# Layer 1 of a four-layer graph network: fill in chunk order, own rows fetched later, score rows spread inside the loop, last block in halves

## The chip, the cores and the metric

The kernel runs on one core of a Trainium2 chip. The core has a matrix engine (TensorE, PE in the profile; its weight loads are shown as PEld), three engines for elementwise work (VectorE = DVE, ScalarE = ACT, GpSimd = POOL), a sync engine (SP) that issues transfers, and 16 DMA engines that move the data. Each engine works through its own queue of instructions in order and waits on semaphores for the others. POOL also issues the indirect transfers, which gather rows by a list of indices.

The metric is the device time of one execution in microseconds (us), as the median of several runs. Lower is better.

## The reference

A matrix `x` of 2708 nodes by 512 features goes through four layers over the same sparse adjacency matrix `adj` (2708 x 2708, about four neighbours per node besides the diagonal). Each layer is followed by `x = layernorm(x + layer(x))`. The change concerns layer 1:

```python
def _L1_gnn_ref(x, adj_a, adj_b, W_sa, a_sa, W_gcnb, b_gcnb, Wa, ba, Wb, bb):
    type_sum_a = adj_a @ x
    type_sum_b = adj_b @ x
    attn_a = sigmoid(concat([type_sum_a, x], 1) @ Wa.T + ba)
    attn_b = sigmoid(concat([type_sum_b, x], 1) @ Wb.T + bb)
    h = x @ W_sa
    s_left, s_right = h @ a_sa[0, :Hd], h @ a_sa[0, Hd:]
    scores = s_left[:, None] + s_right[None, :]
    e = where(adj_a != 0, exp(-leaky_relu(scores, 0.01)), 0.0)
    x_a = (e / (e.sum(1, keepdims=True) + 1e-05)) @ h
    x_b = adj_b @ (x @ W_gcnb) + b_gcnb
    return sigmoid(attn_a * x_a + attn_b * x_b)
```

Layers 0, 2 and 3 are a graph convolution, a hypergraph mean and a symmetrically normalized convolution with a tanh.

## The kernel before, in words

**Tiling.** The nodes are cut into NB = 24 blocks of R = 113 rows. For each block the kernel holds a list of at most 512 edges, in EC = 4 chunks of 128. One chunk is one indirect transfer (`gather`, L604): 128 partitions each receive the table row of one edge's source node. The sum over neighbours is then four matmuls per output half, one per chunk, with a 128 x 113 matrix that has each edge's value (or score) at the column of its target row.

**Layer 1's table.** Layer 0 ends by writing `table[0]` to DRAM: for each node 1029 numbers (4116 bytes), that is `h`, `x @ W_gcnb`, and a few columns for the scores and gates. `store0` writes its windows; the last one, of 20 rows, is the last thing that layer 0 puts there. Layer 1 then needs, for every block, four gathered chunks (into one of NGB = 3 buffers `gath`) and the block's own rows of the table (diagonal terms), which lie in one of NO = 9 places (`own_place`). `load_own1` fetches own rows with plain transfers from SP's queue; `gather_own1` (L1396) does so with one indirect transfer from POOL's queue.

**The fill.** In layer 0's last steps the own rows of blocks 0 to 3, then 4 to 6 are fetched by `load_own1`, and after the last `store0` those of blocks 7 and 8. Then come set-up operations on VectorE (`ediag`, `gates`, `inverse`, `in_block`, `block_of`), `gather1(0)` and `gather1(1)` on POOL, the edge matrices of both blocks on ScalarE (`values1`), and six `spread_left` (L1376 on): each takes the column `s_left` of four blocks and spreads it by four PE transposes (L1380) into a PSUM tile `sl`, from which VectorE copies it (L1383) as a row over all partitions. There are two such PSUM buffers. `spread_bias` (L1559, L1560) does the same for the bias. Then `scores1(0)` (L1424 to L1429) and `mask1(0)` (L1434) make the scores of block 0.

**The loop.** The schedule is written by hand (`manual_schedule`): each engine runs its instructions in program order. Step i does, in this order:

- `gather1(i + 2)` on POOL;
- `sums1(i)` on PE (L1441, tile `l1s`): the plain sums, first all four chunks of the first output half, then of the second;
- `both1(i - 1)` on VectorE (L1486 to L1497, tiles `rec`, `l1a`, `l1v`) and a tanh on ScalarE (L1501): it joins the two branches of the block before;
- `scored_sums1(i)` on PE (L1451, tile `l1e`). There is one PSUM buffer for it, so it waits for `l1a` of block i - 1;
- `scores1(i + 1)`, which needs all four chunks of block i + 1;
- `gather_own1(i + 8)` on POOL for steps 1 to 15;
- `stats1(i - 1)` (L1506 to L1522; in every second step POOL raises the variances of two blocks to the power -0.5, L1523);
- `gates1(i)` and `gated1(i)` (L1461 to L1480, tile `l1b`): ScalarE copies two columns to `row_cnt` (L1465) ahead of the long VectorE operation L1471;
- `mask1(i + 1)`, `scale1`, `norm1(i - 2)`, whose rows SP stores to `table[1]`, and `source_sum(i)` (L1352), a small VectorE operation.

**The end.** After step 23 `both1(23)`, `stats1(23)`, `norm1(23)` finish the last block: VectorE and ScalarE take turns on tiles 512 wide. Layer 2 gathers from `table[1]`, so its first gather waits for the last store.

Of the kernel before, what the change touches and what calls it, by code (L numbers as in the profile page):

```python
# [447 lines left out]
def sparse_stack(  # L448
# [199 lines left out]
    def load_own1(i):  # L648
        r = rows(i)
        own1[i] = own_place(i)  # L650
        move_rows(
            r, lambda a, b: own1[i][a:b, 1 : 2 * D + 1],
            lambda a, b: table[0][i * R + a : i * R + b, 1 : 2 * D + 1],
        )
# [7 lines left out]
    with ExitStack() as phase:  # L662
# [632 lines left out]
                    load_own1(i)  # L1295
        keep_busy(4)
        store0(KB - 1)
        for i in range(7, NO):
            load_own1(i)


    gpool = ctx.enter_context(tc.tile_pool(name="gpool", bufs=1))
# [26 lines left out]
    for k, t in enumerate((ba_bc, bb_bc)):  # L1329
# [4 lines left out]
    nc.vector.reciprocal(inverse, inverse)  # L1334


    in_block = gpool.tile([P, NB, NS], I32, name="in_block")
    nc.vector.tensor_scalar(
        in_block, where_all, 1.0 / R, 0.5 / R - 0.5, op0=ALU.mult, op1=ALU.add
    )  # L1340
    block_of = gpool.tile([P, NB, NS], FP, name="block_of")
    for g, (c0, _) in enumerate(SEGS):
        at = slice(8 * g, 8 * g + 8)
        nc.vector.tensor_scalar(
            block_of[:, :, at], in_block[:, :, at], float(c0), None, op0=ALU.add
        )
    deg_k = gpool.tile([P, KB], FP, name="deg_k")

    def source_sum(b):
# [68 lines left out]
                bias=edges[:, i, c, 1:2], scale=nvalue[:, i, c : c + 1],  # L1418
            )

    def scores1(i):

        e = spool.tile([P, EC, R], FP, tag="e", name=f"e{i}")
        nc.vector.tensor_tensor(  # L1424
            e, gath[i % NGB][:, :, SR : SR + 1].to_broadcast([P, EC, R]),
            over_chunks(s_left[:, i, :]), ALU.add,
        )
        nc.vector.scalar_tensor_tensor(e, e, 0.01, e, op0=ALU.mult, op1=ALU.max)
        nc.scalar.activation(e, e, AF.Exp, scale=-1.0)  # L1429
        edge_e[i] = e  # L1430

    def mask1(i):
        e = edge_e[i]
        nc.vector.scalar_tensor_tensor(e, edge_s[i], 0.0, e, op0=ALU.is_gt, op1=ALU.mult)  # L1434

    def sums1(i):
        g, s, r = gath[i % NGB], edge_s.pop(i), rows(i)
        sum_s[i] = ps_1s.tile([P, 2, D], FP, tag="s1", name=f"l1s{i}")
        for k, at in enumerate(s_at):
            for c in range(EC):  # L1440
                nc.tensor.matmul(  # L1441
                    sum_s[i][:r, k, : at.stop - at.start], lhsT=s[:, c, :r], rhs=g[:, c, at],
                    start=(c == 0), stop=(c == EC - 1),
                )

    def scored_sums1(i):
        g, e, r = gath[i % NGB], edge_e.pop(i), rows(i)
        sum_e[i] = ps_1e.tile([P, 2, D], FP, tag="e1", name=f"l1e{i}")
        for k, at in enumerate(e_at):
            for c in range(EC):  # L1450
                nc.tensor.matmul(  # L1451
                    sum_e[i][:r, k, k : k + at.stop - at.start], lhsT=e[:, c, :r],
                    rhs=g[:, c, at], start=(c == 0), stop=(c == EC - 1),
                )

    def gates1(i):

# [21 lines left out]
        )  # L1479
        nc.scalar.activation(vb[:r, :], vb[:r, :], AF.Copy, scale=gate[:r, 1:2])  # L1480

    def both1(i):

        r, agg = rows(i), sum_e.pop(i)
        rec = small.tile([P, 1], FP, tag="rec", name=f"rec{i}")
        nc.vector.scalar_tensor_tensor(  # L1486
            rec[:r, :], agg[:r, 0, 0:1], 1e-5, ediag[:r, i : i + 1], op0=ALU.add, op1=ALU.add
        )
        nc.vector.reciprocal(rec[:r, :], rec[:r, :])
        nc.vector.tensor_mul(rec[:r, :], rec[:r, :], gate1.pop(i)[:r, 0:1])  # L1490
        va = work.tile([P, D], FP, tag="u", name=f"l1a{i}")
        nc.vector.scalar_tensor_tensor(  # L1492
            halves(va, r), halves(own1.pop(i)[:, 1 : D + 1], r), ediag[:r, i : i + 1],
            agg[:r, :, 1 : H + 1], op0=ALU.mult, op1=ALU.add,
        )
        v = work.tile([P, D], FP, tag="v", name=f"l1v{i}")
        nc.vector.scalar_tensor_tensor(  # L1497
            v[:r, :], va[:r, :], rec[:r, :], vb1.pop(i)[:r, :], op0=ALU.mult, op1=ALU.add
        )

        nc.scalar.activation(v[:r, :], v[:r, :], AF.Tanh, scale=0.5)  # L1501
        v1[i] = v

    def stats1(i):
        r, v = rows(i), v1[i]
        nc.vector.scalar_tensor_tensor(  # L1506
            v[:r, :], v[:r, :], 0.5, xr[:r, i, :], op0=ALU.mult, op1=ALU.add
        )
        stats = small.tile([P, 6], FP, tag="stats", name=f"st_l1_{i}")
        nc.vector.bn_stats(stats[:r, :], v[:r, :])  # L1510
        k = i % 2
        if k == 0 or i >= NB - 2:
            mv2[0] = small.tile([P, 2, 4], FP, tag="mv4", name=f"mv_l1_{i}")
        mv = mv2[0]
        nc.vector.bn_aggr(mv[:r, k, 0:2], stats[:r, :])
        v1[i] = v, mv[:, k, :]
        if k == 0 and i < NB - 2:
            return

        at = slice(k, k + 1) if i >= NB - 2 else slice(0, 2)  # L1520
        n = at.stop - at.start
        nc.vector.tensor_scalar(mv[:r, at, 1], mv[:r, at, 1], 1e-5, None, op0=ALU.add)  # L1522
        nc.gpsimd.tensor_tensor(  # L1523
            mv[:r, at, 2], mv[:r, at, 1], root[:r, :].to_broadcast([r, n]), ALU.pow
        )
        unscaled[0] = r, mv, at
# [60 lines left out]

    plus = const.tile([P, NB], FP, name="plus")
    inv_norm = const.tile([P, NB], FP, name="inv_norm")
    nc.vector.tensor_scalar(plus, adiag, 0.0, None, op0=ALU.is_gt)  # L1590

    def row_norms(at, on_pool=True):
        n = at.stop - at.start
# [41 lines left out]
    values1(0, range(EC))  # L1635
    gather1(1)
    values1(1, range(EC))
    for i in range(0, NB, 4):
        spread_left(i)
    spread_bias(bg_bc)  # L1640
    scores1(0)
    mask1(0)
    for i in range(NB):
        if i + 2 < NB:
            gather1(i + 2)
        sums1(i)
        if i > 0:
            both1(i - 1)
        if i + 2 < NB:
            values1(i + 2, (0, 1))  # L1650
        scored_sums1(i)
        if i + 1 == NB:
            turn_norm(0)
            turn_norm(1)
        if i + 1 < NB:
            scores1(i + 1)
        if 0 < i and i - 1 + NO < NB:
            gather_own1(i - 1 + NO)
        if 0 < i < NB - 1:
            stats1(i - 1)  # L1660
        gates1(i)
        if i + 2 < NB:
            values1(i + 2, (2, 3))
        gated1(i)
        if i + 1 < NB:
            mask1(i + 1)
        else:
            stats1(i - 1)
        scale1()
        if i > 1:  # L1670
            norm1(i - 2)
        if i + 1 == NB:
            norm1(i - 1)
        if i + 1 == NB:
            nc.sync.dma_start(out=b3_bc[0:1, :], in_=b3[None, :])
            nc.sync.dma_start(out=w3_sb, in_=w3T.rearrange("(b p) o -> p b o", p=P))
        if i < KB:
            source_sum(i)
        if i == KB:
            source_sums_out()  # L1680
            row_norms(slice(0, KB))
    copy_norm(0)
    copy_norm(1)
    keep_warm(ps_sp, "sp", [P, 4, P], 8)
    both1(NB - 1)
    spread_row(b3_bc, "b3")
    stats1(NB - 1)
    scale1()
    norm1(NB - 1)
    deg_ps = source_sums_in()  # L1690
# [234 lines left out]
```

## Time and profile before

| | us |
|---|---|
| median of 3 runs | 958.26 (957.83 to 959.23) |
| the profiled execution | 958.69 |
| its span, first to last instruction | 956.9 |
| PE busy | 884.8 (92%) |
| VectorE busy | 685.3 (72%) |
| ScalarE busy | 526.3 (55%) |
| POOL busy | 465.5 (49%) |
| first gather of layer 1 issued | 414.26 |
| first scored sums of layer 1's last block | 603.17 |
| first gather of layer 2 issued | 618.51 |

The shares are means over stages with different limits: layer 0 fills the span to about 414 us, layer 1 goes to 618, layer 2 to about 760, layer 3 to the end. What the change is worth has to be read from the stage it touches. A line of the view in order of time has start, duration, engine, line of the kernel, operation, output<-input, shape, count, and in brackets the idle time of the engine ahead of it with what ended it. The list of waits has who waited for whom, microseconds in total, times, and the longest. `issue` means that the engine waited for nothing that the profile shows.

### The profile page before, as it was taken

The page shows a single profiled execution, that of the slowest core. Times are in us where ns is not written, and L with a number is a line of the kernel's source. Part 1 is how long each engine was busy: PE and PEld are TensorE (multiplying, and loading weights), DVE is VectorE, ACT ScalarE, POOL GpSimd, SP SyncE. Part 2 cuts the span into 40 slices and gives each one's busy share as a digit, 9 for nine tenths or more (in the row PEclk, how much of TensorE's full clock was granted, in tenths as well). Part 3 has the DMA queues.
Part 4 walks back from the last instruction along what each step waited for, and adds up shares of the span by engine and source line. Part 5 has one row for each costly group of instructions (what it writes and reads, how often), then busy time and mean ns, then how long its engine had stood idle before and what let it go on. Part 6 is the DMA issues. An engine that isn't in the chain of part 4 may idle for free.

```text
span 956.9 us, 11163 instructions
## 1 busy us (share of the span) xinstructions
PE 884.8 (92%) x2957; PEld 489.4 (51%) x2957; DVE 685.3 (72%) x1811; ACT 526.3 (55%) x1221; POOL 465.5 (49%) x518
## 2 busy tenths in 40 slices
PE   6889999999999999989999999798888899999993
PEld 2446565556565565557777777433233334444441
DVE  7788798888888853148999999777777436565553
ACT  5776676867677672347777777344544312222221
POOL 3323131432323230057777753377777477766630
PEclk7879999999999999989999999989999999999997
DMA  9986887988878454388999976367777466555531
GB/s 245 323 208 184 216 229 207 272 223 220 227 206 238 152 166 126 115 286 292 349 330 342 341 276 236 95 188 213 212 218 217 131 170 189 163 174 162 151 107 32
DMA packets 133717, 201.73 MB, mean 211 GB/s; under 512 B 82658, under 2 KB 82704, under 8 KB 133647
## 3 DMA queue, kind: packets, MB, share of 16 engines
q0 software_dynamic: 39024, 118.69, 40.2%
q1 hardware_dynamic: 94623, 82.25, 30.2%
q8 instruction: 26, 0.43, 0.2%
q14 instruction: 44, 0.36, 0.1%
HBM read 182.81 MB, written 27.80 MB: 220 GB/s over the span
## 4 chain that ended last, share of the span: by engine, by line
PE 58%; DMA 14%; DVE 14%; issue 5%; ACT 4%; SPq 3%; POOL 2%; POOLq 0%; DVEq 0%; ACTq 0%
PE o_l L588 15%; DMA gath<-table,source 11%; PE l3a L617 8%; PE hb L588 7%; PE h L588 7%; PE l0a L617 6%; PE l2a L617 2%; PE fetched L929 2%; POOL gath L604 2%; PE unread L1585 2%; DVE l1b L1471 1%; SPq L691 1%; DMA gath<-in_x_dram 1%; DVE l1b L1475 1%; DVE l1a L1492 1%
## 5 line engine op out<-in xcount | busy, mean ns | idle before, releaser
L604 POOL DMA_INDIRECT gath<-table,source x288 | 305.0, 1059 | 102.7 <-issue 49.0
L604 POOL DMA_INDIRECT gath<-in_x_dram,source x96 | 97.4, 1015 | 224.9 <-issue 190.7
L617 PE MATMUL l2a<-gath,s_left 128*113 128x512 f32 (+1 forms) x192 | 97.2, 624 | 17.6 <-DMA gath<-table,source 17.4
L1451 PE MATMUL l1e<-gath,e 128*113 128x257 f32 (+3 forms) x384 | 88.4, 383 | 10.4 <-DVE l1a L1492 10.4
L617 PE MATMUL l3a<-gath,s 128*113 128x512 f32 (+1 forms) x192 | 88.3, 603 | 2.7 <-DMA gath<-table,source 2.7
L1441 PE MATMUL l1s<-gath,s 128*113 128x256 f32 (+3 forms) x384 | 89.8, 387 | 0.0
L617 PE MATMUL l0a<-gath,s 128*113 128x512 f32 (+1 forms) x192 | 87.5, 596 | 0.1
L588 PE MATMUL o_l<-shared,xi_own 128*113 128x512 f32 (+1 forms) x192 | 86.5, 593 | 0.8 <-ACT xi_own L581 0.7
L588 PE MATMUL hb<-w_gc_sb,xi_own 128*128 128x512 f32 (+1 forms) x176 | 83.3, 601 | 0.0
L1451 PEld LDWEIGHTS l1e<-gath,e 128*113 128x113 f32 (+1 forms) x384 | 66.2, 177 | 32.7 <-PE l1s L1441 19.4
L588 PE MATMUL o_l<-w_sb,uw_own 128*128 128x512 f32 (+1 forms) x176 | 82.7, 614 | 0.2
L588 PE MATMUL h<-w_sa_sb,xi_own 128*128 128x259 f32 (+1 forms) x352 | 80.8, 382 | 0.0
L1441 PEld LDWEIGHTS l1s<-gath,s 128*113 128x113 f32 (+1 forms) x384 | 69.2, 181 | 17.8 <-ACT s L1416 1.5
L588 PEld LDWEIGHTS h<-w_sa_sb,xi_own 128*128 128x128 f32 (+1 forms) x352 | 64.8, 185 | 19.8 <-issue 6.1
L617 PEld LDWEIGHTS l2a<-gath,s_left 128*113 128x113 f32 (+1 forms) x192 | 30.4, 181 | 73.9 <-DMA gath<-table,source 53.9
L1844 ACT ACTIVATE y<-l3v,mv_l 113x512 f32<-113x512 f32 (+1 forms) x24 | 19.5, 813 | 86.2 <-DVE mv_l L1840 79.2
L588 PEld LDWEIGHTS o_l<-shared,xi_own 128*113 128x113 f32 (+1 forms) x192 | 33.9, 177 | 49.2 <-issue 47.1
L617 PEld LDWEIGHTS l0a<-gath,s 128*113 128x113 f32 (+1 forms) x192 | 33.5, 179 | 40.7 <-issue 35.5
L617 PEld LDWEIGHTS l3a<-gath,s 128*113 128x113 f32 (+1 forms) x192 | 32.5, 180 | 41.2 <-issue 37.9
L1818 DVE SCALAR_TENSOR_TENSOR l3v<-o_l,d_inv,b_bc 113x512 f32<-113x512 f32 (+1 forms) x25 | 18.1, 728 | 48.1 <-PE o_l L588 48.1
L1308 DVE TENSOR_SCALAR s<-niota_r,nrow,edges 128x113 f32<-128x113 f32 x192 | 51.5, 344 | 0.0
L876 DVE FIND_INDEX8 where_all<-rec_all,shared 128x8 uint32<-128x678 f32 (+1 forms) x64 | 51.2, 800 | 0.0
(256 smaller groups left out, 1580.6 us busy)
## 6 DMA issues: line engine op xcount, KB each, us to landing
shared<-in_adj_dram SPq DMA_DIRECT2D x14, 1186.5 KB
table<-st SPq DMA_DIRECT2D x21, 514.5 KB
gath<-in_adj_dram SPq DMA_DIRECT2D x7, 1186.5 KB
gath<-in_x_dram SPq DMA_DIRECT2D x21, 256.0 KB
xi_own<-in_x_dram SPq DMA_DIRECT2D x23, 224.0 KB
table<-xr SPq DMA_DIRECT2D x23, 224.0 KB
table<-y SPq DMA_DIRECT2D x23, 224.0 KB
out_dram<-y SPq DMA_DIRECT2D x23, 224.0 KB
```

The source lines that it names most:

```text
L588: nc.tensor.matmul(o, lhsT=uT[:, f, :r], rhs=w[:, f, :], start=(f == 0), stop=(f == DB - 1))
L604: nc.gpsimd.indirect_dma_start(out=g[:, c, :n], out_offset=None, in_=src[:, :], in_offset=bass.IndirectOffsetOnAxis(ap=source[:, i, c : c ...
L617: nc.tensor.matmul(agg[:r, :], lhsT=s[:, c, :r], rhs=g[:, c, off : off + D], start=(c == 0), stop=(c == EC - 1),)
L691: nc.sync.dma_start(out=a[:TAIL, NF, :r], in_=adjT[NF * P :, at])
L876: nc.vector.max_index(out=where_all[:, i, g * 8 : (g + 1) * 8], in_max=top, in_values=seg)
L929: nc.tensor.matmul(t["fetched"][:, c, : 3 * NS], lhsT=t["q"][:, c * P : (c + 1) * P], rhs=rec_all[:, i].rearrange("p k s -> p (k s)"), sta ...
L1308: nc.vector.tensor_scalar(s[:, c, :], niota_r, nrow[:, i, c : c + 1], edges[:, i, c, 1:2], op0=ALU.is_equal, op1=ALU.mult,)
L1441: nc.tensor.matmul(sum_s[i][:r, k, : at.stop - at.start], lhsT=s[:, c, :r], rhs=g[:, c, at], start=(c == 0), stop=(c == EC - 1),)
L1451: nc.tensor.matmul(sum_e[i][:r, k, k : k + at.stop - at.start], lhsT=e[:, c, :r], rhs=g[:, c, at], start=(c == 0), stop=(c == EC - 1),)
L1585: nc.tensor.matmul(o[:, :cols], lhsT=ident, rhs=bg_bc[:, :cols], start=True, stop=True)
L1818: nc.vector.scalar_tensor_tensor(v[:r, at], o[:r, at], d_inv[:r, i : i + 1], b3_bc[:r, at], op0=ALU.mult, op1=ALU.add,)
L1844: nc.scalar.activation(y[:r, :], v[:r, :], AF.Identity, bias=mv[:r, 3:4], scale=mv[:r, 2:3])
```

## The change

1. The plain transfers of the own rows of blocks 7 and 8 after the last `store0` go. `gather_own1` fetches six blocks ahead, so it starts with block 7 in step 1 and goes on to step 17.
2. `spread_left` runs for blocks 0 to 7 in the fill; the other four calls stand in steps 1 to 4 of the loop, ahead of `source_sum`.
3. Block 0's scores and masks are made in two halves (chunks 0 and 1, chunks 2 and 3), and its matmuls go chunk by chunk over both output halves. Other blocks keep their order.
4. `in_block`, `block_of` and `plus` are computed after `spread_bias`. Two matmuls whose result nobody reads stand ahead of `spread_bias`.
5. The last block's `both1` and `stats1` work on two halves of 256 columns.

Most of the diff's text only moves functions ahead of the fill. Its core:

```diff
         store0(KB - 1)
-        for i in range(7, NO):
-            load_own1(i)
...
-    def scores1(i):
+    def scores1(i, at=slice(0, EC)):
+        if i not in edge_e:
+            edge_e[i] = spool.tile([P, EC, R], FP, tag="e", name=f"e{i}")
+        e, n = edge_e[i][:, at, :], at.stop - at.start
...
-    def mask1(i):
+    def mask1(i, at=slice(0, EC)):
+        e = edge_e[i][:, at, :]
...
+    def in_turn(i, parts):
+        both = [(k, at, c) for k, at in enumerate(parts) for c in range(EC)]
+        return sorted(both, key=lambda t: t[2]) if i == 0 else both
...
-        for k, at in enumerate(s_at):
-            for c in range(EC):
+        for k, at, c in in_turn(i, s_at):
...
-    def both1(i):
+    def both1(i, parts=2):
+        for k in range(0, 2, parts):
+            kk, at = slice(k, k + parts), slice(k * H, (k + parts) * H)
+            nc.vector.scalar_tensor_tensor(
+                halves(va, r)[:, kk, :], halves(own, r)[:, kk, :], ediag[:r, i : i + 1],
+                agg[:r, kk, 1 : H + 1], op0=ALU.mult, op1=ALU.add,
+            )
+            nc.vector.scalar_tensor_tensor(
+                v[:r, at], va[:r, at], rec[:r, :], vb[:r, at], op0=ALU.mult, op1=ALU.add
+            )
+            nc.scalar.activation(v[:r, at], v[:r, at], AF.Tanh, scale=0.5)
...
-    def stats1(i):
+    def stats1(i, parts=1):
+        for k in range(parts):
+            at = slice(k * D // parts, (k + 1) * D // parts)
+            nc.vector.scalar_tensor_tensor(
+                v[:r, at], v[:r, at], 0.5, xr[:r, i, at], op0=ALU.mult, op1=ALU.add
+            )
+            nc.vector.bn_stats(stats[:r, k, :], v[:r, at])
...
-    for i in range(0, NB, 4):
+    for i in (0, 4):
         spread_left(i)
+    unread = ps_1s.tile([P, 2, D], FP, tag="s1", name="unread")
+    for _ in range(2):
+        nc.tensor.matmul(
+            unread[:, 0, :], lhsT=ident[:R, :], rhs=xr[:R, 0, :], start=True, stop=True
+        )
     spread_bias(bg_bc)
...
-    scores1(0)
-    mask1(0)
+    for at in (slice(0, 2), slice(2, EC)):
+        scores1(0, at)
+        mask1(0, at)
     for i in range(NB):
...
-        if 0 < i and i - 1 + NO < NB:
-            gather_own1(i - 1 + NO)
+        if 0 < i and i + 6 < NB:
+            gather_own1(i + 6)
...
+        if 0 < i and 4 * i + 4 < NB:
+            spread_left(4 * i + 4)
         if i < KB:
             source_sum(i)
...
-    both1(NB - 1)
+    both1(NB - 1, 1)
     spread_row(b3_bc, "b3")
-    stats1(NB - 1)
+    stats1(NB - 1, 2)
```

## The prediction

> **What bounds the kernel now.** The profiled execution took 958.69 us, of which 956.9 are span and 1.8 lie around it; the median of the runs shown is 958.26 (957.83 to 959.23). I add my terms to 958.69 and move the result down by 0.43 to stand beside the median. One execution differs from the next by about 0.2%, so below 0.2% (1.9 us) I call a difference "within".
>
> The change touches layer 1 alone: its fill (from about 414 to 434 us), its loop of 24 blocks (to about 604) and its last block (to 617). I read the loop first, in the view of stages (us, then busy us of PE, PE's weight loads, VectorE, ScalarE, POOL, PE clock, DMA share, GB/s), and in the list of waits between 430 and 600 us (who waited for whom, us in total, times, longest).
>
> ```profile
> 430.00:550.00 120.00, 113.17 (x507) 88.11 (x506) 109.21 (x283) 91.24 (x232) 92.16 (x86) 1.00 0.94 331
> 550.00:596.00 46.00, 43.13 (x194) 33.63 (x193) 42.05 (x110) 35.66 (x91) 23.66 (x24) 1.00 0.77 266
> ```
> ```profile
> PE l1e L1451 <- DVE l1a L1492: 9.7, 22, 0.6
> DVE l1b L1471 <- ACT row_cnt L1465: 7.7, 23, 0.7
> ```
>
> VectorE is busy 91% in both stretches, and the only idle time that the list gives it is the 0.3 us a step in which ScalarE reads `row_cnt`. It never waits for a transfer or for PE; PE waits for VectorE, 22 times. In the instructions in order of time, `l1a` (L1492) starts at 449.41 and 456.89: the step is 7.5 us, 7.8 in the next, 15.3 for two. Own-row fetches stop at 545 us, POOL's work and the DMA share fall, and the pace stays: POOL's pair-wise power op starts at 537.87, 553.14 and 568.46. So **VectorE sets the loop**, and whatever is added to its queue there is paid.
>
> The fill is the opposite. In order of time (start, duration, engine, line, in brackets the idle time before it):
>
> ```profile
> 414.26 1.01 POOL L604 DMA_INDIRECT gath<-table,source  x1 [0.43 <-issue]
> ...
> 416.20 1.16 DVE L1383 COPY s_left<-sl 128x452 f32<-128x452 f32 x2
> ...
> 419.06 0.63 DVE L1383 COPY s_left<-sl 128x452 f32<-128x452 f32 x1 [0.33 <-PE sl L1380]
> ...
> 423.34 0.99 POOL L604 DMA_INDIRECT gath<-table,source  x1 [0.30 <-issue]
> 424.33 0.63 DVE L1424 TENSOR_TENSOR e<-gath,s_left 128x452 f32<-128x452 f32 x1 [1.52 <-DMA gath<-table,source]
> ...
> 429.35 0.63 DVE L1424 TENSOR_TENSOR e<-gath,s_left 128x452 f32<-128x452 f32 x1 [2.46 <-DMA gath<-table,source]
> ```
>
> VectorE waits here for transfers: 1.52 us for block 0's last chunk, 2.46 for block 1's. POOL issues a chunk every 1.3 us from 414.26 without a stop, the eighth at 423.34, and it lands 5.9 us later (median issue to landing of the eight: 5.9). From 429.35 VectorE runs through step 0 and reaches the first `l1a` at 434.17. **Only the landing of chunk 8 and VectorE's work behind it set the fill's end**; the sums of block 0 on PE are not on that path.
>
> **The change, part by part.**
>
> *Block 0 by chunks.* The sums of block 0 are put in chunk order, and its scores are made in two halves: three more VectorE operations, one more ScalarE. A half-length operation keeps a fixed part: in layer 3 the row of the 512-wide `l3v` has 0.751, of the 256-wide 0.477, so 2 x 0.477 - 0.751 = 0.2 fixed. Three of them are 0.6 us, in VectorE's 4.0 us of idle. On PE the first sums end earlier than 431.38 (where block 0's scored sums end now), but the next VectorE instruction that needs them comes after 429.35 anyway: the gate at 430.57 waits for nothing now, and the sums' first long user, at 431.43, waits for ScalarE. Gain 0; POOL's fetch of block 3, now held by 0.36 us at 430.36 for a buffer, starts at its usual 0.30, but no one waits for it. If the cover failed, 0.6 us.
>
> *Moved set-up.* `in_block` and `block_of` (0.50 and 0.83) go behind the bias copy, into the same idle time; four of the six spreads leave the fill, which makes room for them: 0. The two added unread matmuls stand on PE where it is idle for 2.45 us before 416.87: 0.
>
> *No own rows in the fill.* Four SP transfers go (two blocks, 0.93 MB, issued 411.44 to 412.79). They could hold up the chunks only by sharing the DMA engines. Bytes by queue between 415.3, when the first chunk's issue ends, and 417 us (q1 is SP's queue, q0 POOL's):
>
> ```profile
> q0 software_dynamic: 42, 0.17, 49.9%
> q1 hardware_dynamic: 58, 0.17, 36.9%
> ```
>
> After 416.5 q0 is alone. So 0.17 MB of own rows compete; at 0.33 MB/us (331 GB/s in the loop) that is 0.5 us. The bounds: 0, if the 5.9 us belong to the chunks themselves when they follow each other at 1.3 us (the fourth and the eighth both have it, though the own rows had long ended); 1.5, if all chunks came down to the 4.4 of the first chunk after a DMA pause, at 584.69. I take **-0.5**, since the bytes are what was seen. The tail of the table store, which releases POOL's queue at 413.56, was issued before those transfers and shares engines with them: 0 to -0.3, taken as 0.
>
> The Trainium skill, "DMA: Bandwidth & Descriptors", section "Anatomy of one DMA — SWDGE (gpsimd) path", gives about 2.0 us plus bytes over 436 GB/s for one such transfer. With 128 rows of 4116 bytes that is an estimate of 3.2 us, 4.2 with the 1.0 us of issue, where this trace has 5.9; by the rule the fill would gain 1.7 and not 0.5, and the whole sum would come out 1.2 lower.
>
> *Own rows six ahead.* Steps 1 to 15 issue one own fetch each, as before; steps 16 and 17 get one more each, 1.3 us of POOL with the gap. POOL has room there:
>
> ```profile
> 553.14 0.71 POOL L1523 TENSOR_TENSOR mv_l<-mv_l,root 113x2 f32<-113x2 f32 x1 [2.26 <-DVE gate L1461]
> ...
> 568.46 0.72 POOL L1523 TENSOR_TENSOR mv_l<-mv_l,root 113x2 f32<-113x2 f32 x1 [3.86 <-DVE gate L1461]
> ```
>
> And the loop held its pace with own fetches before 550. Cost 0; without that cover 2.6. SP gets nothing new.
>
> *Spreads in steps 1 to 4.* Each adds four transposes on PE, between the scored sums and the next sums, and one copy on VectorE ahead of the source sum. PE: eight transposes took 0.94 (413.48 to 414.42), so 0.47 a step; PE waits 0.3 to 0.6 for `l1a` each step, and `l1a` itself comes later by the copy, so this is covered. VectorE: two copies took 1.16 where one takes 0.62, so one more costs 0.54 in a full queue. The copy adds a wait on PE: behind it stand the source sum, then `rec` and `l1a`, for which PE waits. In step 2 the scored sums end at 446.2 and the transposes would at 446.7; the copy's turn is the source sum's, 448.67. So 2 us of slack, no wait. 4 x 0.54 = **+2.2**. In the fill the copies cost nothing, in the loop they cost all of it. The bounds: 0, if the loop is in truth paced by POOL (it issues with 0.30 us gaps from 447 to 550, and a chunk landed at 458.07 for an operation at 458.40, 0.3 in hand); 3.8, if each copy pays its whole 0.63 and the 0.33 that one waited for PE in the fill. I stay at 2.2, by the two-copy row.
>
> *Last block by halves.* Now the chain from `l1a` at 609.30 to the aggregate at 613.05 takes 3.75. Its half-wide relatives in layer 3:
>
> ```profile
> L1818 DVE SCALAR_TENSOR_TENSOR l3v<-o_l,d_inv,b_bc x25: 477/751/753, 778.2 to 943.4; 113x512 f32<-113x512 f32 x23, 109x256 f32<-109x256 f32 x2
> L1822 ACT ACTIVATE l3v<-l3v x25: 416/630/631, 780.4 to 943.9; 113x512 f32<-113x512 f32 x23, 109x256 f32<-109x256 f32 x2
> L1828 DVE TENSOR_TENSOR l3v<-l3v,xr x25: 407/684/695, 781.1 to 944.8; 113x512 f32<-113x512 f32 x23, 109x256 f32<-109x256 f32 x2
> L1829 DVE BATCH_NORM_STATS2 st_l<-l3v x25: 426/695/696, 781.8 to 945.2; 113x6 f32<-113x512 f32 x23, 109x6 f32<-109x256 f32 x2
> ```
>
> With 0.49, 0.42, 0.43, 0.43 and the gaps of the present chain (0.11 before `l1v`, 0.04 between dependent ones, 0.08 overlap of independent ones): first half 609.30 to 610.39, second 610.31 to 611.40, then add 611.32, statistics 611.78, add 612.13, statistics 612.60, aggregate 613.06. The 0.70 us that VectorE idled for the tanh is filled, and VectorE's four added fixed parts (0.8) eat it: 0, bounds -0.3 (the overlap everywhere) and +0.3 (one gap of 0.11 more at three places).
>
> Sum: -0.5 + 2.2 + 0 = **+1.7**: 960.4 beside the profiled execution, **959.9** beside the median.
>
> **The rivals.**
>
> A, as worked out: 959.9. For it: VectorE's list of waits. Its own range is +0.6 to +2.7, across the 1.9 line.
>
> B, slower: the copies wait for PE. Place: the spread copy in steps 1 to 4, behind transposes that stand behind the scored sums in PE's queue. Price: 4 x (0.63 + 0.33) = 3.8, and no gain in the fill: 962.1. It decides once the transposes end over 2 us later than worked out, as with PE at half clock (0.85 and 0.72 granted from 414 to 430). Against it: clock 1.00 from 430 on.
>
> C, faster: the loop is paced by POOL's issues and the landings, and the copies hide; the fill gives all its bounds, -1.5, -0.3 and the tail -0.3: -2.1, 956.2. For it: POOL's gapless issue. Against: VectorE waited for no landing in 22 steps.
>
> D, the parts do nothing: no transfer gain, copies hidden: 958.3. Against it the same list.
>
> **How the numbers follow.** A 0.60 (0.42 within, 0.18 slower), B 0.20 (slower), C 0.14 (0.10 faster, 0.04 within), D 0.06 (within). That is faster 0.10, within 0.52, slower 0.38. The range must leave out no more than 0.2: from 957.4, inside C (-0.9: copies hidden and half of the fill's bounds), to 962.0, B nearly whole.
>
> **What would show it.** Right: block 1's score operation some 0.5 us earlier than 429.35, four copies of 0.6 in steps 1 to 4 with no idle time ahead of them, the steps there 8.0 to 8.3 apart, the others unchanged, the last block's chain at 3.7. Wrong: VectorE with idle time behind landings in the loop (C), idle time ahead of the copies (B), or a latency near 4.4 for all eight chunks, which makes the fill worth three times my figure.

## The result and the profile after

The changed kernel takes 963.41 us (median of 18 runs, 958.53 to 968.81) beside 959.07 for the kernel before (18 runs, the three shown ahead among them): ratio 1.0039, interval 1.0025 to 1.0054. The prediction of 959.9 and its range up to 962.0 were too low. The profiled execution took 964.88 us, 963.2 of them span.

I set the two traces side by side by landmarks, single instructions that both kernels have. "Store" is the issue of the last store of the table in layer 0, "fetch" the first gather of a layer, "step" the distance of two `l1a`:

| us | before | after |
|---|---|---|
| start to store (layer 0) | 411.02 | 414.82 |
| store to layer 1's first fetch | 3.23 | 2.81 |
| fetch to first `l1a` | 19.92 | 19.92 |
| steps 1 to 4 | 30.48 | 32.61 |
| the other steps | 144.65 | 144.50 |
| last `l1a` to layer 2's first fetch | 9.21 | 9.04 |
| **store to layer 2's first fetch** | **207.48** | **208.87** |
| layer 2's first fetch to layer 3's | 142.29 | 141.53 |
| layer 3's first fetch to the last statistics | 184.44 | 185.82 |
| to the end | 11.65 | 12.12 |

Layer 1 is 1.4 us longer, near the +1.7 of the prediction. The other 4.9 of the 6.3 us between the spans lie in layers that the change does not touch.

First layer 1, by the views of the prediction. Stages (columns as there), shifted by 3.4 us with the fill's end:

```profile
433.40:553.40 120.00, 111.54 (x503) 87.27 (x502) 109.42 (x282) 90.54 (x232) 91.58 (x84) 0.99 0.92 326
553.40:599.40 46.00, 43.21 (x194) 33.71 (x193) 42.03 (x112) 35.78 (x92) 28.05 (x28) 1.00 0.85 298
```

VectorE is as busy as before, 91%. Its own list of waits in the loop, 437 to 607 us, is one line, the one that it had:

```profile
DVE l1b L1465 <- ACT row_cnt L1459: 7.0, 22, 0.3
```

POOL, by its pair-wise power op, still has room in the steps that the prediction named (0.45 us, where it had 2.26, and 2.27, where it had 3.86):

```profile
558.60 0.71 POOL L1522 TENSOR_TENSOR mv_l<-mv_l,root 113x2 f32<-113x2 f32 x1 [0.45 <-DVE gate L1455]
...
573.85 0.72 POOL L1522 TENSOR_TENSOR mv_l<-mv_l,root 113x2 f32<-113x2 f32 x1 [2.27 <-DVE gate L1455]
```

In order of time, step 1 of the loop (the step began with the `l1a` at 437.55):

```profile
443.73 0.62 DVE L1423 SCALAR_TENSOR_TENSOR e<-s,e 128x452 f32<-128x452 f32 x1
444.26 0.62 DVE L1371 COPY s_left<-sl 128x452 f32<-128x452 f32 x1
444.80 0.35 DVE L1340 SCALAR_TENSOR_TENSOR in_block<-block_of,rec_all 128x192 int32<-128x192 f32 x1
...
445.54 0.74 DVE L1490 SCALAR_TENSOR_TENSOR l1a<-shared,ediag,l1e 113x512 f32<-113x512 f32 x1
```

The copy has no idle time ahead of it, and what follows starts 0.54 later: the step takes 7.99 where it took 7.46. Steps 2 to 4 take 8.29, 7.99 and 8.34; step 5 is back at 7.47.

The fill, VectorE's waits for chunks:

```profile
424.09 0.46 DVE L1414 TENSOR_TENSOR e<-gath,s_left 128x226 f32<-128x226 f32 x1 [0.88 <-issue]
...
427.56 0.40 DVE L1414 TENSOR_TENSOR e<-gath,s_left 128x226 f32<-128x226 f32 x1 [1.61 <-DMA gath<-table,source]
...
432.72 0.63 DVE L1414 TENSOR_TENSOR e<-gath,s_left 128x452 f32<-128x452 f32 x1 [3.43 <-DMA gath<-table,source]
```

The halves of block 0 are done long before block 1's last chunk. That chunk, issued at 426.72, lands 5.88 us later (5.89 before). The first one lands after 4.35 (5.28 before). Bytes by queue behind the first chunk's issue, 418.65 to 420.35 us, show that the own rows are gone and the chunks move no more than before (0.17 MB there):

```profile
q0 software_dynamic: 38, 0.16, 52.7%
```

So the missing own rows did nothing for the eighth chunk. The first lands sooner, but nobody waits for it, and a later trace of the kernel before (e5), with the own rows in place, has 4.24 for it too. The 0.42 that the fill gains lie ahead of it, in the store that lands sooner.

The last block, from `l1a` to the aggregate 3.60 (3.75 before), with no idle time left on VectorE:

```profile
614.66 0.47 DVE L1490 SCALAR_TENSOR_TENSOR l1a<-w_sb,ediag,l1e 109x256 f32<-109x256 f32 x1
...
616.56 0.42 DVE L1506 SCALAR_TENSOR_TENSOR l1v<-l1v,xr 109x256 f32<-109x256 f32 x1
...
618.26 0.21 DVE L1514 BATCH_NORM_AGGREGATE mv_l<-st_l 109x2 f32<-109x12 f32 x1
```

### The profile page after: what moved, and what is told of

The parts are those of the page before. It is cut to its first block, busy times and chain, and to the rows that moved or that the text cites. A ratio compares the mean times of both kernels' runs of the same rounds, so it can differ in the third digit from the quotient of the medians.

```text
span 963.2 us, 11141 instructions
## 1 busy us (share of the span) xinstructions
PE 885.8 (92%) x2961; PEld 488.3 (51%) x2961; DVE 686.1 (71%) x1818; ACT 526.5 (55%) x1223; POOL 468.8 (49%) x520
## 4 chain that ended last, share of the span: by engine, by line
PE 59%; DMA 14%; DVE 11%; ACT 4%; issue 4%; POOL 4%; SPq 2%; POOLq 0%; DVEq 0%; ACTq 0%
PE o_l L588 16%; DMA gath<-table,source 11%; PE l3a L617 9%; PE hb L588 7%; PE h L588 7%; PE l0a L617 6%; POOL gath L604 3%; PE l2a L617 3%; SPq L691 2%; PE fetched L929 2%; PE unread L1584 2%; PE l1e L1445 2%; DMA gath<-in_x_dram 2%; DVE l1b L1465 1%; PE l1s L1436 1%
## 5 line engine op out<-in xcount | busy, mean ns | idle before, releaser
L1445 PE MATMUL l1e<-gath,e 128*113 128x256 f32 (+3 forms) x384 | 89.8, 387 | 12.2 <-DVE l1a L1490 12.2
L1436 PE MATMUL l1s<-gath,s 128*113 128x261 f32 (+3 forms) x384 | 89.6, 386 | 2.0 <-DMA gath<-table,source 2.0
```

The source lines that it names most:

```text
L1436: nc.tensor.matmul(sum_s[i][:r, k, : at.stop - at.start], lhsT=s[:, c, :r], rhs=g[:, c, at], start=(c == 0), stop=(c == EC - 1),)
L1445: nc.tensor.matmul(sum_e[i][:r, k, k : k + at.stop - at.start], lhsT=e[:, c, :r], rhs=g[:, c, at], start=(c == 0), stop=(c == EC - 1),)
```

## The experiments

Two theories to begin with. T1: the change costs what layer 1 shows, the rest is scatter. T2: it also slows stages that it does not touch. Runs of one group share a chip and the runs of the kernel before; the groups are e1 to e4, e5 to e8, e9 to e12, and e13 with e14.

### The spreads, undone and alone; the own rows alone

**e1_after_again** is the changed kernel. 

> The changed kernel once more, unaltered. Theory T1 (the price is the four copies in VectorE's full queue, 4 x 0.53 = 2.1 us, less 0.4 that the fill gains and 0.1 of the last block; what layers 0, 2 and 3 differ by in one pair of profiles is scatter): layer 1, from the last table store to layer 2's first gather, takes 208.9 us in the changed kernel as in its first profile (207.5 before), and layer 0 need not be 3.8 us late again. Theory T2 (the change also slows stages that it does not touch by about 2 us): the last table store comes near 414.8 again, not near 411.0, and the time is about 3.7 us over the kernel before.

**e2_after_spreads_in_fill** takes the spreads back into the fill:

```diff
-    for i in (0, 4):
+    for i in range(0, NB, 4):
         spread_left(i)
...
-        if 0 < i and 4 * i + 4 < NB:
-            spread_left(4 * i + 4)
```

> The changed kernel with all six spreads back in the fill. T1: steps 1 to 4 return to 7.5 and 7.8 us, layer 1 from the last table store to layer 2's first gather is 2.1 us shorter than in the changed kernel, about 206.8, that is 0.6 shorter than before the change; the time is 0.5 us below the kernel before, within 0.2%. T2: layer 1 the same, but the time stays some 1.5 us above the kernel before.

**e3_before_spreads_in_loop** does that part alone in the kernel before (the same lines the other way round). 

> The kernel before with only the four spreads moved into steps 1 to 4. T1: the steps 1 to 4 are 0.53 us longer each, layer 1 2.1 us longer (209.6 from the last table store to layer 2's first gather), the time 2.1 us above the kernel before. T2: the same, as long as layers 0, 2 and 3 stay put; if this kernel also has its last table store near 414.8, moving code alone shifts layer 0.

**e4_before_no_own_in_fill** has only the change of the own rows in the kernel before:

```diff
-        for i in range(7, NO):
-            load_own1(i)
...
-        if 0 < i and i - 1 + NO < NB:
-            gather_own1(i - 1 + NO)
+        if 0 < i and i + 6 < NB:
+            gather_own1(i + 6)
```

> The kernel before with only the own rows moved out of the fill (fetched six ahead in the loop). T1: the time from the last table store's issue to the first l1a, 23.2 us before, falls by 0.4 us, all of it because the store lands sooner; the eighth chunk still needs 5.9 us from issue to landing; the loop's steps stay 7.5 and 7.8. The rival of the prediction (all chunks at 4.4) would give 1.5 to 1.9 us. The time is within 0.2% of the kernel before.

Measured against 970.8 us for the kernel before: e1 0.9997 (0.9967 to 1.0028), e2 0.9985 (0.9956 to 1.0015), e3 1.0008 (0.9981 to 1.0034), e4 0.9994 (0.9967 to 1.0020). In this group every kernel takes about 970, and the layer 2 of all four traces is 150 to 152 us long, not 142; differences of 1 us drown. The traces tell more. Steps 1 to 4 together: e1 32.63 and e3 32.67, with the copies in the loop; e2 30.49, without. So the copies cost 2.1 us there, undone as alone. Store to first fetch: 2.80 to 2.82 in e1, e2 and e4, 3.07 in e3. So the own rows account for that gain, but its size is not sure: the kernel before has 3.23 in its first trace and 2.93 in e5. Two expectations failed. From the store to the first `l1a` e4 takes 23.23, where 22.8 was expected, and layer 1 takes 210.84, 207.65 and 210.32 in e1, e2 and e3, 0.7 to 1.9 over what was expected. Most of that is the way from the first fetch to the first `l1a`: 20.40 to 20.43 in e2, e3 and e4, with the own rows and without, where before and after have 19.92, and 21.84 in e1. There VectorE stood 1.45 us in step 0 for PE:

```profile
436.66 0.16 DVE L1480 SCALAR_TENSOR_TENSOR rec<-l1e,ediag 113x1 f32<-113x1 f32 x1 [1.45 <-PE l1s L1436]
```

In the traces of before, after and e2 to e4 this instruction has no idle time ahead of it. From 10 to 15 us behind the fetch PE's granted clock was 0.69 in e1 and 1.00 in the changed kernel's first trace; that this is the reason is not shown. In e4 the other expectation failed for one step: step 4 took 8.86 and not 7.8, with VectorE waiting 1.0 us for a chunk.

### Which engine copies, and how often

**e5_before_again** is the kernel before as a control. 

> The kernel before, unaltered, as a control and for its profile on this chip. T1 (the change's price is the four copies in steps 1 to 4, 2.1 us, less 0.4 in the fill and 0.1 in the last block; what is beyond that is scatter of stages that the change does not touch): ratio 1.000 with an interval of about 0.3% either way, loop steps of 7.5 and 7.8 from the first on, the last table store of layer 0 anywhere between 408 and 415 us. T2 (the change also slows untouched stages by some 2 us): the same for this run, and it gives the stages of layers 0, 2 and 3 that T2 has to find longer in the changed kernel.

**e6_after_third** is the changed kernel again. 

> The changed kernel, unaltered, a third time. T1: ratio between 1.000 and 1.003 (the 1.4 us of layer 1 are 1.0015, and the chips' scatter stands beside it); steps 1 to 4 0.53 us longer each than in the kernel before; layers 0, 2 and 3 differ from the kernel before by as much as two profiles of one kernel do. T2: ratio 1.004 again, and layers 2 and 3 longer by 1 to 2 us than in the kernel before of this call.

**e7_after_copies_on_scalar** and **e8_after_copies_five_times**, each from the changed kernel:

```diff
-        nc.vector.tensor_copy(s_left[:, i : i + n, :], ps[:, :, :R])
+        copy = nc.scalar.copy if i > 4 else nc.vector.tensor_copy       # e7
+        copy(s_left[:, i : i + n, :], ps[:, :, :R])
...
+        for _ in range(5 if i > 4 else 1):                              # e8
+            nc.vector.tensor_copy(s_left[:, i : i + n, :], ps[:, :, :R])
```

> The changed kernel, but the four spread copies of steps 1 to 4 are made by ScalarE and not by VectorE. T1 (VectorE sets the loop, so what leaves its queue is gained whole): steps 1 to 4 back at 7.46, 7.78, 7.48, 7.77; time 2.1 us below the changed kernel, ratio to the kernel before 0.997 to 1.000. The rival (the transposes on PE or their landing in the step are what costs, not the copy): the steps stay at 7.99 and 8.29, whichever engine copies.

> The changed kernel, with each of the four spread copies of steps 1 to 4 done five times over on VectorE (the same values again). T1: each step grows by four more copies of 0.53 to 0.58 us, so steps 1 to 4 take about 10.2, 10.5, 10.2 and 10.5, 8.6 us more in all than in the changed kernel, and the time shows it in full: ratio to the kernel before 1.008 to 1.012. The rival (part of a longer step is given back later, as the fetches get further ahead): the time grows by clearly less than the steps do, and later steps come out under 7.5 or the stages behind the loop shorter.

Measured against 958.79: e5 1.0007 (0.9990 to 1.0024), e6 1.0026 (1.0012 to 1.0040), e7 1.0028 (1.0009 to 1.0047), e8 1.0144 (1.0126 to 1.0163).

e8, step 1:

```profile
438.51 0.62 DVE L1424 SCALAR_TENSOR_TENSOR e<-s,e 128x452 f32<-128x452 f32 x1
439.05 3.27 DVE L1372 COPY s_left<-sl 128x452 f32<-128x452 f32 x5
442.24 0.35 DVE L1340 SCALAR_TENSOR_TENSOR in_block<-block_of,rec_all 128x192 int32<-128x192 f32 x1
```

The steps take 10.66, 10.95, 10.64 and 10.96: 2.65 for four copies more, 0.66 each and not 0.54. Each copy writes where the last one wrote and starts 0.03 us behind its end, where two that write to different places overlap by 0.08. In all 10.6 us; the time grew by 11.9 over e6's. Nothing is given back: VectorE sets the pace, shown by dose. In e7 the copy stands in ScalarE's queue (441.58, 0.52 long) and steps 1 to 4 take 30.94, 1.7 less than e6's 32.65 (2.2 were expected; step 3 took 7.93 and not 7.5). Layer 1 is 207.53 there. That part held, and e7's time shows nothing of it: I had expected 0.997 to 1.000. In the control e5 I found why a step can eat what a copy saves. The waits of its VectorE in the loop (434 to 604 us), and then those of e7:

```profile
DVE l1b L1471 <- ACT row_cnt L1465: 7.0, 22, 0.3
DVE e L1424 <- DMA gath<-table,source: 1.3, 1, 1.3
```

```profile
DVE l1b L1466 <- ACT row_cnt L1460: 7.0, 22, 0.3
DVE l1v L1495 <- DVE l1a L1491: 0.5, 1, 0.5
DVE e L1415 <- DMA gath<-table,source: 0.4, 1, 0.4
```

In e5 step 4 takes 9.17: a chunk comes late for VectorE. It took 6.99 us to land, about as in the first trace of the kernel before (6.93), but was issued 1.6 us later behind the first `l1a`. The trace that I predicted from had 0.3 us in hand at that place. So the kernel before sometimes pays 1.4 us there; the changed kernel did not in after, e1 and e6 (8.34 each). That its VectorE comes later there is a likely reason, not a shown one. e5's layer 1 is 208.68, e6's 208.85.

Then T2's stages. From layer 3's first fetch to the end, before and e5 need 196.09 and 196.04; after, e6, e7 and e8 need 197.94, 198.03, 198.26 and 197.90. That is no scatter. The difference sits at two places: from the second to the third block's statistics, 6.90 and 6.90 against 8.65, 8.65, 8.64 and 8.64, and from the last statistics to the end, 11.65 and 11.65 against 12.12 four times. What stands at the first is on POOL, in the kernel before and in the changed one:

```profile
789.38 1.00 POOL L604 DMA_INDIRECT gath<-table,source  x1 [0.30 <-PE l3a L617]
791.46 0.99 POOL L604 DMA_INDIRECT gath<-table,source  x1 [1.08 <-issue]
```

```profile
790.20 1.01 POOL L604 DMA_INDIRECT gath<-table,source  x1 [0.30 <-PE o_l L588]
791.24 0.26 POOL L1850 TENSOR_SCALAR mv_l<-mv_l 113x1 f32<-113x1 f32 x1
791.59 0.57 POOL L1851 TENSOR_TENSOR mv_l<-mv_l,root 113x1 f32<-113x1 f32 x1
794.87 1.15 POOL L604 DMA_INDIRECT gath<-table,source  x1 [2.71 <-issue]
```

POOL waits for nothing that the trace shows ("issue"), 2.50 us up to its next instruction of any kind, where it was 0.88 before. Counted from the start of the program, the fetch ahead of the stall is the **325th indirect fetch of POOL in both**. The change puts the own rows of blocks 7 and 8 into POOL's queue (401 fetches and not 399), so the same stall meets layer 3 two fetches earlier. This is a third theory, T3. The traces of the first group agree in the stall: 2.5 in e1, e2 and e4 (e4 has that edit alone), 0.88 in e3. In their times it cannot be seen: from layer 3's first fetch to its last statistics they take 186.25, 186.67 and 188.75, and e3 187.70, with other steps longer as well.

POOL also raises layer 3's variances to the power -0.5 (`mv_l`), behind its fetches, and that is how the stall reaches PE. From the chain of work that ended last, in the changed kernel:

```profile
798.93 1.00 POOL gath L604
...
800.29 0.58 POOL mv_l L1851
...
801.10 0.67 DVE l3v L1835
...
801.86 0.53 ACT xi_own L581
...
802.43 3.69 PE o_l L588 x8
```

The same view of the kernel before, from 782 to 806 us, has no POOL in it. Not all of the 1.75 stays: the next steps are a little shorter, and up to the last statistics layer 3 takes 184.44 and 184.40 in before and e5, and 185.82, 185.91, 186.14 and 185.78 in after, e6, e7 and e8. So 1.4 us are left.

The second place is something else. Up to SP's last store, 3.2 us behind the last statistics, both kernels keep the same distances. Then POOL closes the program with a `DRAIN` (count, then shortest, median and longest in ns; before, then after):

```profile
L1920 POOLq DRAIN  x3: 40/107/6684, 949.4 to 956.6; - x3
L1937 POOLq DRAIN  x3: 40/107/6847, 955.5 to 962.9; - x3
```

The long one takes 6.68 us with 399 indirect fetches in the program, 6.77 with 400, 6.85 with 401 and 5.46 with 384, in all 16 traces: 0.08 us a fetch. With the instruction ahead of it, 0.04 longer, that makes 0.2 of the 0.47. The other 0.27 stand behind a branch of POOL ahead of both; what makes them stays open.

### The stall moved on purpose

**e9_after_own_78_on_sp** sends blocks 7 and 8 through SP's queue, **e10_after_own_all_on_sp** all own rows of the loop, and **e11_own_on_sp_spreads_in_fill** is e10 with e2's edit:

```diff
-            gather_own1(i + 6)
+            (load_own1 if i + 6 < NO else gather_own1)(i + 6)           # e9
...
+            load_own1(i + 6)                                            # e10, e11
```

> The changed kernel, but the own rows of blocks 7 and 8 are fetched in steps 1 and 2 through SP's queue and not POOL's, so that POOL's queue holds as many indirect fetches as in the kernel before (399 and not 401). T3 (two more fetches in POOL's queue move a stall of POOL, which stands behind its 325th indirect fetch in every trace so far, two fetches earlier in layer 3, where it lasts 2.50 us and not 0.88 and costs that layer 1.75, and the end of the program another 0.46): the stall is back at 0.88, the time between the second and the third block's statistics of layer 3 is 6.9 and not 8.65, the stretch from the last statistics to the end 11.65 and not 12.1; layer 1 as in the changed kernel, steps 1 to 4 at 8.0 and 8.3; time 2 us under the changed kernel's, ratio 0.999 to 1.002. The rival (layer 3 is longer for another reason of the changed kernel, such as where its instructions lie): the stall and the 8.65 stay. The second rival (all of it is scatter): neither holds to a pattern.

> The changed kernel, but all own rows that the loop fetches go through SP's queue; POOL's queue has 384 indirect fetches. T3: the stall behind the 325th fetch comes 17 fetches later than in the changed kernel, in layer 3's fifth or sixth step, and not in the second; there POOL is ahead of PE's pace by about 1 us a step, so that at most 1.5 of its 2.5 us are seen; the third block's statistics follow the second's after 6.9 us or less. In layer 1, POOL has 17 times 1.3 us less to issue, which no step shows, as VectorE sets the pace. Time 1 to 3 us under the changed kernel's. The rival (position does not matter): a step of 8.65 stays in layer 3's third block.

> All that the runs have shown to be worth it: the changed kernel with all six spreads in the fill (as before the change) and all own rows of the loop through SP's queue. T1 with T3: steps 1 to 4 at 7.5 and 7.8, the fill 0.4 shorter than in the kernel before, the last block 0.15 shorter, layer 3 without the step of 8.65 and without part of the stall that the kernel before has: 0.5 to 2.5 us under the kernel before, ratio 0.997 to 1.000. The rival (the spreads in the fill now delay block 0's halves): the first l1a comes later against the first fetch than the 19.9 us of the changed kernel.

**e12_after_without_parts** makes block 0 and the last block whole again:

```diff
-        return sorted(both, key=lambda t: t[2]) if i == 0 else both
+        return both
...
-    for at in (slice(0, 2), slice(2, EC)):
-        scores1(0, at)
-        mask1(0, at)
+    scores1(0)
+    mask1(0)
...
-    both1(NB - 1, 1)
+    both1(NB - 1)
-    stats1(NB - 1, 2)
+    stats1(NB - 1)
```

> The changed kernel without its two parts by pieces: block 0's sums and scores are made whole, as before the change, and so is the last block's normalization. T1 (neither is on a path that ends late, or gains what it costs): from the first fetch to the first l1a 19.9 us as with the chunks, and the last block's chain from l1a to the aggregate 3.75 and not 3.60; time within 0.5 us of the changed kernel. The rival (the chunks of block 0 leave PE with short idle times and lower its clock, so that block 1's sums end later): the fill is shorter by 0.3 us or more.

Measured against 957.40: e9 1.0034 (1.0018 to 1.0050), e10 1.0125 (1.0101 to 1.0150), e11 1.0113 (1.0090 to 1.0136), e12 1.0048 (1.0025 to 1.0071).

e9's POOL behind the 325th fetch:

```profile
788.27 1.00 POOL L604 DMA_INDIRECT gath<-table,source  x1 [0.30 <-PE l3a L617]
790.35 1.00 POOL L604 DMA_INDIRECT gath<-table,source  x1 [1.08 <-issue]
```

The stall is back at 0.88, the step at 6.90 and layer 3 at 184.47 up to its last statistics, as T3 said; the end took 11.92, not quite half of the way back, as two fetches less make of the `DRAIN`. Layer 3 to the end is 196.39. The ratio was expected at 0.999 to 1.002 and is 1.0034, so that expectation failed. Beside e12, which is the changed kernel but for its two parts by pieces, e9's median is 2.1 us lower (960.06 and 962.18), but the two intervals overlap. Part of the reason is in the trace: SP, with nothing ahead of it, issued the two blocks at once, in the fill; the first chunk landed after 6.7 and not 4.2, the eighth after 6.4 and not 5.8, and the fill took 20.40 and not 19.85.

In e10 and e11 the stall again stood behind the 325th fetch, now between layer 3's fifth and sixth statistics, 1.67 long, and layer 3 to the end took 195.01 and 194.82, a us less than in the kernel before. All of that is the shorter `DRAIN`: up to the last statistics they take 184.61 and 184.42, no less than the kernel before. The time still went up by 11.5 us, against my expectation. e10's VectorE in the loop, 434 to 604 us, and then the queues and the chunk fetches of that stretch (packets, MB, share of the engines; number, median us to landing):

```profile
DVE e L1414 <- DMA gath<-table,source: 6.5, 8, 1.4
```

```profile
q0 software_dynamic: 11793, 38.24, 67.1%
q1 hardware_dynamic: 4508, 11.49, 21.0%
gath<-table,source POOLq DMA_INDIRECT x80, 7.7
```

In e6 the chunks took 6.5 there and q1 had 7.2%. SP's queue brings a block of own rows at one blow beside the chunks and no longer in turn with them, and VectorE now waits for landings 8 times (11.3 us in e11). That the engines' sharing makes the chunks late is my reading; the later landing and the waits are measured. The Trainium skill, "SBUF — State Buffer", section "SBUF: two separate sides", advises to move transfers from GpSimd's queue to SP's or ScalarE's when VectorE keeps GpSimd from writing descriptors. No run here shows that blocking by itself; these two speak against the remedy in this loop.

e12: fetch to first `l1a` 19.86, with block 0 whole as by chunks; the last block's chain 3.76 and not 3.60, and last `l1a` to layer 2's first fetch 9.17 against 9.04. The parts by pieces are worth 0 and 0.15. That the time stays within 0.5 us of the changed kernel's could not be read: no unaltered changed kernel stands in this group.

### The last two

What was still open then: whether the position of the stall alone sets its cost, and whether the change's gains can be had without its costs. **e13_best_of_both** is e2 with blocks 7 and 8 on SP behind a store; **e14_after_one_own_on_sp** is the changed kernel with only block 7 there:

```diff
-        if 0 < i and i + 6 < NB:
+        if 2 < i and i + 6 < NB:        # e13; in e14: 1 < i
             gather_own1(i + 6)
...
         if i > 1:
             norm1(i - 2)
+        if i in (2, 3):                 # e13; in e14: i == 2
+            load_own1(i + 5)
```

> The changed kernel with all six spreads in the fill, as before the change, and the own rows of blocks 7 and 8 through SP's queue, each behind the store of a normalized block in steps 2 and 3, so that they neither meet block 0's chunks nor stand in POOL's queue (399 indirect fetches). T1 with T3: from the last table store to the first l1a 0.4 us less than in the kernel before (22.7 and not 23.1), steps 1 to 4 at 7.5 and 7.8, the last block's chain 3.60, POOL's stall in layer 3 0.88 long and the third block's statistics 6.9 us behind the second's; 0.5 us under the kernel before, which the ratio can't tell from 1 (0.998 to 1.001). The rival (a wait in the loop takes it back, such as the stall of 1.4 us that a profile of the kernel before had in step 4): a step over 8 among steps 1 to 4.

> The changed kernel with one of its two added own fetches taken off POOL's queue (block 7's own rows go through SP's queue, behind the store in step 2; block 8's stay with POOL): 400 indirect fetches. T3: the stall stands behind the 325th fetch again, one fetch earlier in layer 3 than in the kernel before and one later than in the changed kernel; its length lies between 0.88 and 2.50, and the stretch from the second to the third block's statistics between 6.9 and 8.65. The rival (only the number of instructions of the changed kernel matters, not the fetches): 2.50 and 8.65 as in the changed kernel.

Measured against 957.25: e13 1.0025 (1.0014 to 1.0037), e14 1.0061 (1.0043 to 1.0079). e14's POOL:

```profile
787.57 1.15 POOL L604 DMA_INDIRECT gath<-table,source  x1 [0.19 <-PE l3a L617]
790.60 1.00 POOL L604 DMA_INDIRECT gath<-table,source  x1 [1.87 <-issue]
```

With 400 fetches the stall behind the 325th is 1.67 and the step 7.70; with 399 and 401 they are 0.88 and 6.90, 2.50 and 8.65. Each fetch that the stall comes earlier makes that step 0.8 to 0.95 us longer. Up to the last statistics layer 3 takes 184.4 to 184.5 with 399 fetches, 185.3 with 400 and 185.8 to 186.1 with 401, outside the first group. The place sets the cost, not the length alone: in e10 a stall of 1.67 cost nothing that shows. e13 has the shortest way from the store to the first `l1a` of all traces, 22.30 (before 23.15), the stall at 0.88 and no copy in its loop. Yet it falls to its rival, the late chunk:

```profile
DVE e L1414 <- DMA gath<-table,source: 2.5, 2, 1.9
```

Steps 4 and 5 take 9.75 and 8.21. The chunk that step 4 waits for was issued 0.4 us behind SP's block of own rows and landed after 9.1 us. In e14, where SP brings a block at the same place, it took 9.3, and step 4 9.36; in before, after, e5 to e9 and e12, with none there, 6.0 to 7.4. No version that I tried beats the kernel before by more than its interval.

## Why the prediction was wrong

The chance stood mostly on "within" and 963.41 lies outside the range. 0.8 of the 3.5 us that it lies above 959.9 are the kernel before itself, 959.07 over 18 runs and 958.26 over three. Step by step:

- **What bounds the loop**: right. VectorE's list of waits did not change, and e7 and e8 show that what is put into its queue is paid and what is taken out is gained, as long as the chunks come in time.
- **Spreads, +2.2**: right, 2.1 in the trace, 2.2 alone in e3, 2.1 undone in e2.
- **No own rows in the fill, -0.5**: near in size (0.42 in the first pair of traces, 0.1 beside e5), wrong in place. The term stood on the chunks' landing, which did not move (5.89 and 5.88); what moved is the tail of the store, which I had taken as 0, with -0.3 as its bound. Two errors met, and that the size came out near is luck. By the Trainium skill, "DMA: Bandwidth & Descriptors", section "Anatomy of one DMA — SWDGE (gpsimd) path", I had estimated 4.2 us for one chunk. The first of the row now takes 4.35 and comes near it; the eighth, 5.88, does not.
- **Block 0 by chunks, set-up, last block**: 0, 0 and 0. With the first and the last undone, e12 shows 0 and -0.15; the moved set-up was not tried alone.
- **"Own rows six ahead ... Cost 0"**: this is the step that failed. I counted the two added fetches of POOL against the room in the steps that issue them, and "the change touches layer 1 alone" kept me from following POOL's queue further. They move a stall of POOL so that one step of layer 3 takes 1.75 us more, of which 1.4 are left at the layer's end, and they lengthen the closing `DRAIN`, 0.2 of the 0.47 at the end: 1.6 us in place of 0, some 350 us behind the first of them. e9 and e14 show the layer's part, with the fetches undone and by half; e4, with this edit alone, has the stall of 2.5 us.
- **Rival C**, the landings pace the loop: weighed as all or nothing. In some executions it holds for one step, worth 1.4 us in e5's step 4.
- **The range**: it rested on "one execution differs from the next by about 0.2%". The 18 runs of the changed kernel span 10 us. The last store of layer 0, in code that no kernel here changed, lies between 408.03 and 414.82 in 16 traces.

What stays open: by the traces, from the store to the end, the changed kernel needs 548.35 and 548.03 and the kernel before 545.86 and 547.68, 1.4 us on the mean (loop +1.3, layer 3 and end +1.9, layer 2 -1.3, the two ends of layer 1 -0.5). The medians differ by 4.3 us in the runs of the result and 2.6 in e6's group, and by 0.3 in e1's, with an interval of 3 either way. e9 and e13, too, came out 2 to 2.7 above the kernel before, where their traces give 1.2 and 0.4. A profiled execution lay anywhere from 3.3 us below the median of its kernel's runs (e10) to 3.3 above (e1). Two profiles of a kernel are too few against steps that come in some executions and not in others; whether that is all, the runs do not settle. Nor do they settle why layer 2 is shorter (140.97 to 141.84) in all five traces with 401 fetches outside the first group; e13 and e14, with 399 and 400, have 141.54 and 141.51 too. So the stall in layer 3 is shown by experiment, and most of the 4.3 us is not.

## What to carry to other kernels

Count what an edit adds to each queue for the whole program, not for the steps that issue it: a stall that hangs on a queue's count of transfers moves with it and shows far behind the edit. Work put into the queue of the engine that sets the pace is paid in full, and may still be nearly free in an execution where that engine would have waited for a transfer, as e5 suggests. Before calling an effect of 2 us, look at several profiles of each kernel, stage by stage, and take a range from the spread of many runs and not from three.

## What I had not expected of the hardware

- POOL stands still behind its 325th indirect fetch in all 16 traces, whether the program has 384, 399, 400 or 401 of them and whether 742 or 769 recorded instructions stand ahead: 0.88, 1.67 or 2.50 us. In e9, e10, e11, e13 and e14, where a chunk is POOL's 113th fetch, it stands still 1.9 us behind that one too, in step 1 of the loop; in the others an own-row fetch is the 113th and POOL stays idle 0.5 to 4.1 us behind it, mostly put down to PE, so they do not tell. A piece of code (16 KB, instruction queue q8) is fetched 0.5 to 0.9 us behind the stall's end in before, after, e9 and e14, 4.4 us ahead of the stall in e13, and none is near it in e10; so loading of code is not shown to be the cause, and what the cause is stays open.
- POOL's closing `DRAIN` grows by 0.08 us with each indirect fetch of the whole program (5.46 us with 384, 6.85 with 401).
- The same copy costs a full VectorE queue 0.53 us at 0.62 of its own length, and 0.66 when it must wait for the one before it.
- The first chunk fetch of a row lands after 4.35 us (after) or 4.24 (e5), 5.29 in the first trace of the kernel before, and the eighth, 1.3 us apart, after 5.9 to 6.0, with and without 0.93 MB of other rows ahead of them.
